# Gates and second modulation as fused products and sums on VectorE, in a transformer block's first heads

## The chip, the cores and the metric

The kernel runs on one core of a Trainium2 chip. The metric is the device time of one execution in microseconds (us), given as the median of repeated runs. A core has five engines with a queue each, served in order: TensorE (PE, matrix products into the PSUM banks), VectorE (DVE), ScalarE (ACT), GpSimd (POOL), and SyncE (SP), which here only issues transfers (DMAs). Semaphores order the queues among each other.

## The reference

One block with adaptive layer norm, for 2 batches of 1024 tokens of width 256, all in float32. From a small vector `c` per batch come six modulation rows: shift and scale of the attention half (`sa`, `ca`), its gate (`ga`), and the same for the feed-forward half.

```
mod = (silu(c) @ wmod).reshape(2, 6, 1, 256)
sa, ca, ga, sb, cb, gb = mod[:, 0..5]
ga = (2*(ga >= 0) - 1) * maximum(abs(ga), 0.25)          # gb likewise
h = layernorm(x) * (1 + ca) + sa
x = x + ga * attention(h)            # 16 heads of 128, rotary q and k, causal softmax, @ Wo + bo
h = layernorm(x) * (1 + cb) + sb
x = x + gb * ffn(h)                  # quantized weights, silu(gate) * up, 704 hidden
```

## The kernel before

The program is one list of instructions in an order written out by hand (`tc.manual_schedule`); each engine takes its own in that order. There are 32 units, one for each batch and head (`units`, two heads to a weight group), and the main loop goes over a unit's eight steps `i`, one for each block of 128 queries. "Head 0" below is the first unit, "head 1" the second, and so on; `n` is the unit's number.

Step `i` of a unit does the following, in this order. `shared_out` projects one token tile of an earlier unit through its output weight and adds it to `x` (`project_out`, L518 on TensorE, L521 on VectorE); it runs 13 steps behind, so unit 0's first tile comes in step 5 of head 1. `score` (L431) multiplies 128 queries with `(i+1)*128` keys into one of two `ps` banks, and VectorE adds the mask there and reduces to the negative maximum (L434, the fused form `tensor_tensor_reduce`, shown as CUSTOM_DVE_ANT_0 and an accumulator read). `turned` (L465) transposes the previous step's probabilities in 32x32 blocks on VectorE; after steps 3 and 7 SP issues 16 DMAs that complete the transposition into `pT` (L477). `expo` (L451) is the exponential on ScalarE. `release` runs what the last `project_qk` held back: VectorE's product with the cosine (L404) and GpSimd's addition (L407). `project_qk` (L388) projects q or k of the next unit; ScalarE adds the bias into a rotated copy `r` (L400, two buffers), GpSimd multiplies it with the sine (L401). `project_v` (L370, two token tiles at a time, copied out by ScalarE L377) and `values` (L492, the product with v into the single `po` bank, copied out by ScalarE L500) follow, then `extras`.

Before the loop stands a prologue. SP and ACT queue the loads; at most eight of these transfers are on their way at a time, since each takes one of eight semaphores in turn and waits until the one before it on that semaphore has landed. x is normalized (`ln_stats`, `ln_sqrt`, `ln_scale`), transposed by TensorE and modulated into `hT` (`ln_turn`, L218, L226 on VectorE, L224 on ScalarE), in two halves of 512 tokens. Between them stand the products of the modulation on TensorE: `modulation(0)` (L125) for the attention half's shift and scale, which lands as columns, and `gates_product` (L149) for both gates, which lands as two rows of 512. `gates` applies sign and lower bound on these rows with four VectorE operations (L155 to L159), writes them to DRAM through SP and reads them back with four broadcasts to 128 partitions. The feed-forward half's `modulation(2)` is done in step 7 of head 0. `fold_out` (GpSimd, L339 to L343) adds a weight group's share of the value bias and multiplies the output weight by the gate; for the first group in step 7 of head 0, before the first `project_out` reads it.

Of the kernel before, what the change touches and what calls it, by code (L numbers as in the profile page):

```python
# [22 lines left out]
KC = D // P  # L23
HG = 2
# [3 lines left out]
QB = 512  # L28
# [9 lines left out]
def adaln_block(ctx: ExitStack, tc: tile.TileContext, a, cos_d, sin_d, out):  # L38
    nc = tc.nc
    pool = lambda name, bufs, **k: ctx.enter_context(tc.tile_pool(name=name, bufs=bufs, **k))  # L40

    const = pool("const", 1)
# [16 lines left out]

    wmod = fpool.tile([P, 2, 2, KC, D], F32, tag="f", name="wmod")  # L60
    wga = fpool.tile([P, KC, 2 * D], F32, tag="f", name="wga")

    def load_x(b, t, n, eng):
        eng.dma_start(x[b][:, t : t + n, :], x_d[b, :, t : t + n, :])

    def load_wmod(block, n, eng):
        eng.dma_start(wmod[:, block, n], a["L0_wmod"][block, n])

# [7 lines left out]
    for n in range(2):  # L76
        load_wmod(0, n, nc.sync)

# [37 lines left out]

    def modulation(which, pool, tag):

        pm = pool.tile([P, 512], F32, tag=tag, name=f"pm{which}")

        wide = pm.rearrange("p (n f r b) -> p n f r b", n=2, f=KC, b=B)
        for n in range(2):
            for f in range(KC):
                for k in range(KC):
                    nc.tensor.matmul(  # L125
                        wide[:, n, f],
                        wmod[:, which // 2, n, k, ts(f, P)],
                        sc[:, :, k].unsqueeze(1).to_broadcast([P, P // B, B]),
                        start=(k == 0),
                        stop=(k == KC - 1),  # L130
                    )
        pms[which] = wide

    pms = {}

    def shift_scale(which):
        pm = pms[which]
        for n in range(2):
            nc.vector.tensor_scalar(modT[:, which + n], pm[:, n, :, 0, :], float(n), None, ALU.add)

    dram = pool("dram", 1, space=bass.MemoryType.DRAM)
    grow_d = dram.tile([B, 2 * D], F32, name="grow_d")

    pgs = []

    def gates_product(k):
        if k == 0:
            pgs.append(ps_y.tile([P, 512], F32, tag="y", name="pg"))
        nc.tensor.matmul(pgs[0][:B], sc[:, :, k], wga[:, k, :], start=(k == 0), stop=(k == KC - 1))  # L149

    def gates():

        pg = pgs.pop()
        sgn = ppool.tile([P, S], F32, tag="p", name="sgn")[:B, :QB]
        nc.vector.tensor_scalar(sgn, pg[:B], 0.0, 2.0, ALU.is_ge, ALU.mult)  # L155
        mag = ppool.tile([P, S], F32, tag="p", name="mag")[:B, :QB]
        nc.vector.tensor_scalar(mag, pg[:B], -1.0, None, ALU.mult)
        nc.vector.scalar_tensor_tensor(mag, pg[:B], 0.25, mag, ALU.max, ALU.max)
        nc.vector.scalar_tensor_tensor(mag, sgn, -1.0, mag, ALU.add, ALU.mult)  # L159
        nc.sync.dma_start(grow_d, mag)  # L160
        for b in range(B):
            for m, n in enumerate(("a", "b")):
                nc.sync.dma_start(
                    gate[n, b], grow_d[b : b + 1, m * D : (m + 1) * D].to_broadcast([P, D])
                )

# [164 lines left out]

    def fold_out(b, g):
        t = weights[b, g]["o"]
        if b == 0:

            for h in range(HG):
                c = R_BV + g * HG + h
                bw = small.tile([P, D], F32, tag="bw", name=f"bw_{g}{h}", bufs=2)
                nc.gpsimd.tensor_scalar(bw, t[:, h, :], cols[:, c : c + 1], None, ALU.mult)  # L339
                nc.gpsimd.tensor_tensor(bvacc, bvacc, bw, ALU.add)  # L340

        for h in range(HG):
            nc.gpsimd.tensor_tensor(t[:, h, :], t[:, h, :], gate["a", b], ALU.mult)  # L343

    gbo = {}
# [14 lines left out]
    weights = {}  # L360
# [150 lines left out]
    def project_out(u, t, late=False):  # L511
# [5 lines left out]
        py = bank(name) if late else ps_y.tile([P, 512], F32, tag="y", name=name)  # L517
# [130 lines left out]
    def extras(n, i):  # L648

        if i == (2 if n else 7) and units[n][2] == 0:  # L650
            fold_out(*units[n][:2])
        if n == 0 and i == 7:
            modulation(2, ps_y, "y")
            shift_scale(2)

# [45 lines left out]
    def shared_out(s, late=False):  # L701
        if s >= 0:
            project_out(units[s // NT], s % NT, late)

    with tc.manual_schedule():
        pc = ps_a.tile([P, 512], F32, tag="a", name="pc")
        nc.tensor.transpose(pc[:, : B * KC], row_c, ident[: B * KC, : B * KC])
        for n in range(2):
            warm_up(4)
        nc.scalar.activation(sc.rearrange("p b k -> p (b k)"), pc[:, : B * KC], AF.Silu)  # L710
        nc.scalar.activation(warm, eps_t, AF.Sqrt)
        weights[0, 0] = {}
        nc.sync.dma_start(wga, a["w_gates"])
        load_w(0, 0, "q")
# [6 lines left out]
        for t, t_d in ((cos_t, cos_d), (sin_t, sin_d)):  # L721
            nc.sync.dma_start(t[:, QB:], t_d[:, QB:])
        for n in range(2):
            load_wmod(1, n, nc.sync)
        load_proj(*units[2][:2])
# [10 lines left out]
        modulation(0, ps_o, "o")  # L736
        ln_scale(0, "a", 0, (0, 1))
        ln_scale(0, "a", 0, (2, 3))
        shift_scale(0)
        ln_turn(0, "a", 0, 0, new_hT(0, 0), split=True)  # L740
        gates_product(0)
        for t in range(4, NT):
# [7 lines left out]
        ln_turn(0, "a", 1, 0, new_hT(0, 1), split=True, wide=True)  # L750
        gates_product(1)
        project_v(0, 0, 2, ps_sc, "sc", S)
        gates()
        for s in ("q", "k"):
# [3 lines left out]
        for n, u in enumerate(units):  # L758
# [5 lines left out]
            for i in range(NT):  # L764

                shared_out(8 * n + i - 13)
                if owed:
# [10 lines left out]
                if i in (6, 7) and prev:  # L778
                    values(prev, 1, 4 * (i - 6), 4 * (i - 5))
                if i in (0, 2):  # L780
                    if h == 0:
                        project_v(b, g, 4 + i, *((ps_a, "a") if n else (ps_o, "o")))
                    elif more:
                        project_v(nb, ng, i)
                if not nxt and i in filler:
                    hidden(0, 0, filler.index(i), late=False, hold=True)

                if prev and i == (0 if n > 1 else 2):
                    values(prev, 0, 0, 4)
                extras(n, i)  # L790
                if i == 7 and h == 1:
# [125 lines left out]
```

## Time and profile before

| what | value |
|---|---|
| median of 3 runs | 1073.14 us (1072.92 to 1076.41) |
| the profiled execution | 1074.62 us |
| its span, first to last instruction | 1072.6 us |
| busy: PE, DVE, ACT, POOL | 1067.6, 656.7, 508.8, 399.2 us |
| granted TensorE clock | 1.00 |
| head 0's first score on TensorE | 23.72 us |
| first scores of heads 1, 2, 3 | 43.58, 71.15, 100.42 us |

All times inside the span count from its first instruction. In a line of a timeline the first number is the start, the second the duration in us, then engine, line of the kernel, operation and operands (out<-in, partitions x elements); "x16" is that many instructions merged, and brackets give the idle time of the engine just before and what ended it. In a line of the groups the numbers behind the bar are the total busy time in us and the mean duration in ns. In a line of the transfers the last number is the time from issue to landing in us. PEld is TensorE's loading of weights, which lies beside the products. Durations of matrix products include the depth of the pipeline; what one occupies is the distance to the next start.

### The profile page before, as it was taken

To read this page: it belongs to the slowest core of one execution; us is meant where nothing else is said; L and a number is where in the kernel's file an instruction comes from. 1 tells how busy PE (TensorE), PEld (TensorE's weight loads), DVE (VectorE), ACT (ScalarE), POOL (GpSimd) and SP (SyncE) were. 2 spreads that over 40 slices of the span, in tenths; PEclk is the share of its full clock that TensorE was granted. 3 is DMA by queue.
4 is the path that set the end of the run, shared out by engine and by line. 5 is a ranking of instruction groups with operands and counts; after the bars stand their busy time and mean duration, and the time that the engine had idled before them with its cause. 6 is when DMAs were issued, how large, how long until landed. Compare 5 with 4: busy or idle time off the path is not lost.

```text
span 1072.6 us, 12387 instructions
## 1 busy us (share of the span) xinstructions
PE 1067.6 (100%) x3513; PEld 638.1 (59%) x3513; DVE 656.7 (61%) x1427; ACT 508.8 (47%) x956; POOL 399.2 (37%) x368
## 2 busy tenths in 40 slices
PE   9999999999999999999999999999999999999998
PEld 5655655665665656556666666656556666545746
DVE  5666675666767776655656656666767756545321
ACT  5654454554445544445544444544555544562110
POOL 4735353534344343754333444334343333200100
PEclk9999999999999999999999999999999999999999
DMA  6465656657564555655464655454655556423201
GB/s 223 102 160 127 160 119 139 159 125 177 118 156 105 142 116 130 135 135 137 110 148 109 148 118 144 100 138 100 143 124 116 147 128 138 110 50 77 71 1 39
DMA packets 68191, 132.02 MB, mean 123 GB/s; under 512 B 19318, under 2 KB 23546, under 8 KB 68124
## 3 DMA queue, kind: packets, MB, share of 16 engines
q1 hardware_dynamic: 66340, 126.83, 50.2%
q10 hardware_dynamic: 1736, 4.29, 1.2%
q8 instruction: 28, 0.46, 0.2%
q14 instruction: 39, 0.32, 0.1%
q0 software_dynamic: 48, 0.13, 0.1%
HBM read 25.26 MB, written 2.10 MB: 26 GB/s over the span
## 4 chain that ended last, share of the span: by engine, by line
PE 98%; DMA 1%; DVE 0%; issue 0%; ACT 0%; POOL 0%; ACTq 0%; POOLq 0%
PE ps L431 23%; PE po L492 23%; PE pk L388 10%; PE py L518 10%; PE pq L388 10%; PE pv L370 10%; PE pgu L547 7%; PE pd L611 3%; DMA s_down<-in_scales 1%; PE warm_ps L88 1%; PE pd L601 0%; PE pm L125 0%; PE ptx_a L218 0%; PE pg L149 0%; DVE ps L434 0%
## 5 line engine op out<-in xcount | busy, mean ns | idle before, releaser
L451 ACT ACTIVATE p<-ps,nmax 128x128 f32<-128x128 f32 (+7 forms) x256 | 190.2, 743 | 343.1 <-DVE nmax L434 342.7
L431 PE MATMUL ps<-kT,qT 128*128 128x512 f32 (+3 forms) x768 | 289.5, 486 | 0.0
L434 DVE CUSTOM_DVE_ANT_0 ps<-ps,mask 128x128 f32<-128x128 f32 (+7 forms) x256 | 195.5, 764 | 112.6 <-PE ps L431 111.6
L492 PE MATMUL po<-pT,v 128*128 128x512 f32 (+3 forms) x768 | 263.5, 486 | 0.0
L521 DVE SCALAR_TENSOR_TENSOR x<-py,rden,x 128x256 f32<-128x256 f32 x256 | 122.8, 481 | 222.6 <-PE py L518 219.0
L492 PEld LDWEIGHTS po<-pT,v 128*128 128x128 f32 x768 | 145.7, 190 | 123.4 <-issue 92.8
L401 POOL TENSOR_TENSOR r_q<-r_q,sin_t 128x512 f32<-128x512 f32 x64 | 81.6, 1275 | 362.8 <-ACT r_q L400 348.4
L465 DVE STREAM_TRANSPOSE t<-p 128x128 f32<-128x128 f32 (+7 forms) x256 | 198.2, 774 | 4.8 <-ACT p L451 3.1
L431 PEld LDWEIGHTS ps<-kT,qT 128*128 128x128 f32 x768 | 145.7, 190 | 77.6 <-issue 64.1
L518 PE MATMUL py<-wo,o 128*128 128x256 f32 x512 | 151.3, 380 | 1.0 <-DVE x L521 1.0
L518 PEld LDWEIGHTS py<-wo,o 128*128 128x128 f32 x512 | 92.5, 190 | 79.0 <-issue 53.3
L370 PE MATMUL pv<-wv,hT 128*128 128x256 f32 x512 | 121.1, 379 | 0.0
L388 PE MATMUL pq<-hT,wq 128*128 128x512 f32 x256 | 120.5, 593 | 0.0
L388 PE MATMUL pk<-hT,wk 128*128 128x512 f32 x256 | 120.4, 592 | 0.0
L370 PEld LDWEIGHTS pv<-wv,hT 128*128 128x128 f32 x512 | 94.8, 190 | 19.5 <-issue 1.3
L401 POOL TENSOR_TENSOR r_k<-r_k,sin_t 128x512 f32<-128x512 f32 x64 | 81.4, 1272 | 64.4 <-ACT r_k L400 64.3
L407 POOL TENSOR_TENSOR kT<-kT,r_k 128x512 f32<-128x512 f32 x64 | 81.2, 1269 | 55.3 <-DVE kT L404 40.7
L400 ACT ACTIVATE r_q<-pq,cols 64x512 f32<-64x512 f32 x128 | 87.6, 684 | 22.2 <-PE pq L388 19.8
L407 POOL TENSOR_TENSOR qT<-qT,r_q 128x512 f32<-128x512 f32 x64 | 83.6, 1307 | 36.9 <-DVE qT L404 30.2
L400 ACT ACTIVATE r_k<-pk,cols 64x512 f32<-64x512 f32 x128 | 87.6, 684 | 6.5 <-PE pk L388 1.0
L388 PEld LDWEIGHTS pk<-hT,wk 128*128 128x128 f32 x256 | 48.6, 190 | 48.2 <-issue 44.5
L388 PEld LDWEIGHTS pq<-hT,wq 128*128 128x128 f32 x256 | 46.2, 190 | 33.1 <-issue 30.6
(94 smaller groups left out, 690.7 us busy)
## 6 DMA issues: line engine op xcount, KB each, us to landing
pT<-t SPq DMA_DIRECT2D x512, 128.0 KB, 2.4
pT<-t SPq DMA_DIRECT2D x512, 64.0 KB, 2.0
wq<-in_Wq SPq DMA_DIRECT2D x16, 256.0 KB, 3.1
wk<-in_Wk SPq DMA_DIRECT2D x16, 256.0 KB, 3.9
wv<-in_Wv SPq DMA_DIRECT2D x16, 256.0 KB, 4.3
wo<-in_Wo SPq DMA_DIRECT2D x16, 256.0 KB, 3.0
out<-yo SPq DMA_DIRECT2D x15, 128.0 KB, 1.8
wmod<-in_wmod SPq DMA_DIRECT2D x4, 256.0 KB, 5.5
```

The source lines that it names most:

```text
L370: nc.tensor.matmul(pv[:, ts(j, HG * DH)], hT[b, n][:, k, ts(r, P)], weights[b, g]["v"][:, k, :], start=(k == 0), stop=(k == KC - 1),)
L388: nc.tensor.matmul(pq, weights[b, g][s][:, k, ts(h, DH)], hT[b, n][:, k, :], start=(k == 0), stop=(k == KC - 1),)
L400: nc.scalar.activation(r1[to], pq[of], AF.Identity, bias=cols[of, c : c + 1])
L401: nc.gpsimd.tensor_tensor(r1, r1, sin_t[:, sl], ALU.mult)
L407: nc.gpsimd.tensor_tensor(dst[:, sl], dst[:, sl], r1, ALU.add)
L431: nc.tensor.matmul(ps[:, c:e], qT[:, ts(i, P)], kT[:, c:e], start=True, stop=True)
L434: nc.vector.tensor_tensor_reduce(ps[:, :L], ps[:, :L], mask[:, NT - 1 - i :, :].rearrange("p t k -> p (t k)"), -SCALE, FLT_MAX, ALU.add, A ...
L451: nc.scalar.activation(p[:, :L], ps[:, :L], AF.Exp, bias=nmax, scale=-1.0, accum_out=dens[u][:, i : i + 1])
L465: nc.vector.transpose(t32[blk][:, :, j, : i + 1, :].rearrange("p c k b -> p k c b"), p[:, : (i + 1) * P].rearrange("p (k c a) -> p k c a", ...
L492: nc.tensor.matmul(po[:, off * P :], vs[b, g][:, k, ts(h, DH)], pT[:, off:, :, k, :], start=(k == 0), stop=(k == last),)
L518: nc.tensor.matmul(py[:, :D], outs[u][:, ts(t, P)], weights[b, g]["o"][:, h, :], start=True, stop=True)
L521: nc.vector.scalar_tensor_tensor(x[b][:, t, :], py[:, :D], rdens[u][:, t : t + 1], x[b][:, t, :], ALU.mult, ALU.add)
```

## The change

Only the attention half's shift and scale are still computed on TensorE. Both gates and the feed-forward half's shift and scale are computed on VectorE as dot products: the weights come transposed (`wmT`, 128 output columns on the partitions, the 256 inputs along them), silu(c) comes as one row broadcast to all partitions (`crow`, through DRAM), and `column` multiplies and sums them with one `tensor_tensor_reduce` of 128x256 for each batch. Eight of these (four `column` calls) make the gates in steps 4 to 7 of head 0, eight more the second modulation in steps 3 and 5 of heads 1 and 2. Sign and bound of the gates are then four operations on 128x8. GpSimd's queue sends these columns to DRAM, where they lie as rows, and reads the rows back with broadcasts in steps 1 (attention) and 5 (feed-forward) of head 1. The value bias share stays in step 7 of head 0, the multiplication of the first output weight by the gate goes to step 4 of head 1.

The first out-projection goes from step 5 to step 7 of head 1, and unit 0's tiles catch up in head 2, two of them through the `po` bank. The v projections of the second weight group's first four tiles go to steps 6 and 7 of head 0 (from steps 0 and 2 of head 1), the later ones to step 0 of heads 1 and 2 (the last two from steps 0 and 2 of head 2), and head 2's first value product goes from step 0 to step 2.

```diff
-    wmod = fpool.tile([P, 2, 2, KC, D], F32, tag="f", name="wmod")
-    wga = fpool.tile([P, KC, 2 * D], F32, tag="f", name="wga")
+    wmod = fpool.tile([P, 2, KC, D], F32, tag="f", name="wmod")
+    late_mod = fpool.tile([P, (4 * KC + B) * D], F32, tag="f", name="late_mod")
+    wmT = late_mod[:, : 4 * KC * D].rearrange("p (w n f k) -> p w n f k", w=2, n=2, f=KC)
+    crow = late_mod[:, 4 * KC * D :].rearrange("p (b k) -> p b k", b=B)
...
-    grow_d = dram.tile([B, 2 * D], F32, name="grow_d")
-    def gates_product(k):
-        if k == 0:
-            pgs.append(ps_y.tile([P, 512], F32, tag="y", name="pg"))
-        nc.tensor.matmul(pgs[0][:B], sc[:, :, k], wga[:, k, :], start=(k == 0), stop=(k == KC - 1))
+    crow_d = dram.tile([1, B * D], F32, name="crow_d")
+    grow_d = dram.tile([B, 2, KC, P], F32, name="grow_d")
+    gcol = const.tile([P, B, 2, KC], F32, name="gcol")
+
+    def column(which, n, f):
+        junk = xnp.tile([P, D], F32, tag="xn", name=f"junk{which}{n}{f}")
+        for b in range(B):
+            to = modT[:, 2 + n, f, b : b + 1] if which else gcol[:, b, n, f : f + 1]
+            nc.vector.tensor_tensor_reduce(
+                junk, wmT[:, which, n, f], crow[:, b], 1.0, float(which * n), ALU.mult, ALU.add, to
+            )
 
     def gates():
...
+        g = gcol.rearrange("p b n f -> p (b n f)")
+        sgn = small.tile([P, 4 * B], F32, tag="sgn", name="sgn", bufs=1)
+        nc.vector.tensor_scalar(sgn, g, 0.0, 2.0, ALU.is_ge, ALU.mult)
...
         nc.vector.scalar_tensor_tensor(mag, sgn, -1.0, mag, ALU.add, ALU.mult)
-        nc.sync.dma_start(grow_d, mag)
-        for b in range(B):
-            for m, n in enumerate(("a", "b")):
-                nc.sync.dma_start(
-                    gate[n, b], grow_d[b : b + 1, m * D : (m + 1) * D].to_broadcast([P, D])
-                )
+        with nc.allow_non_contiguous_dma("columns to rows"):
+            nc.gpsimd.dma_start(grow_d.rearrange("b n f p -> p (b n f)"), mag)
+
+    def gate_rows(n):
+        for b in range(B):
+            row = grow_d[b : b + 1, "ab".index(n)].rearrange("b f p -> b (f p)")
+            nc.gpsimd.dma_start(gate[n, b], row.to_broadcast([P, D]))
...
-        if i == (2 if n else 7) and units[n][2] == 0:
+        if n == 0 and i == 7:
+            bias_share(0)
+        if n == 1 and i in (1, 5):
+            gate_rows("ab"[i // 5])
+        if n == 1 and i == 4:
+            fold_gate(0, 0)
+        if n and i == 2 and units[n][2] == 0:
             fold_out(*units[n][:2])
+        if n == 0 and i >= 4:
+            column(0, *divmod(i - 4, 2))
         if n == 0 and i == 7:
-            modulation(2, ps_y, "y")
-            shift_scale(2)
+            gates()
+        if n in (1, 2) and i in (3, 5):
+            column(1, n - 1, i // 4)
...
         nc.scalar.activation(sc.rearrange("p b k -> p (b k)"), pc[:, : B * KC], AF.Silu)
+        nc.scalar.activation(row_c, row_c, AF.Silu)
+        nc.gpsimd.dma_start(crow_d.rearrange("o (r p) -> (o r) p", p=P), row_c)
         nc.scalar.activation(warm, eps_t, AF.Sqrt)
         weights[0, 0] = {}
-        nc.sync.dma_start(wga, a["w_gates"])
...
+        nc.sync.dma_start(crow.rearrange("p b k -> p (b k)"), crow_d.to_broadcast([P, B * D]))
         for n in range(2):
-            load_wmod(1, n, nc.sync)
+            nc.sync.dma_start(wmT[:, n], a["wmodT"][:, n])
...
-        gates_product(0)
...
-        gates_product(1)
         project_v(0, 0, 2, ps_sc, "sc", S)
-        gates()
...
-                shared_out(8 * n + i - 13)
+                s = 8 * n + i - 13
+                shared_out({0: -1, 1: -1, 2: 0, 3: 1, 4: 2, 5: 4, 6: 5}.get(s, s))
...
                 if i in (0, 2):
-                    if h == 0:
-                        project_v(b, g, 4 + i, *((ps_a, "a") if n else (ps_o, "o")))
-                    elif more:
+                    if n in (1, 2):
+                        if i == 0:
+                            project_v(0, 1, 2 + 2 * n)
+                    elif n == 0:
+                        project_v(b, n, 4 + i, ps_o, "o")
+                    elif h == 0 and n > 2:
+                        project_v(b, g, 4 + i)
+                    elif h and more:
                         project_v(nb, ng, i)
+                if n == 0 and i in (6, 7):
+                    project_v(0, 1, 2 * (i - 6))
...
-                if prev and i == (0 if n > 1 else 2):
+                if prev and i == (0 if n > 2 else 2):
                     values(prev, 0, 0, 4)
+                if s in (4, 6):
+                    project_out(units[0], 3 * s // 2 - 3, pool=ps_o, tag="o")
```

`bias_share` and `fold_gate` are the two halves of `fold_out`; `project_out` takes the pool of its bank as an argument; `modulation` is left with the attention half alone and writes `modT` itself. The host hands over the transposed weights under the name `wmodT`.

More of the change, by code (lines that the diff above doesn't have):

```diff
@@ L58, in adaln_block, with load_wmod @@
     sc = const.tile([P, B, KC], F32, name="sc")
-    wmod = fpool.tile([P, 2, 2, KC, D], F32, tag="f", name="wmod")
-    wga = fpool.tile([P, KC, 2 * D], F32, tag="f", name="wga")
+    wmod = fpool.tile([P, 2, KC, D], F32, tag="f", name="wmod")
+    late_mod = fpool.tile([P, (4 * KC + B) * D], F32, tag="f", name="late_mod")
+    wmT = late_mod[:, : 4 * KC * D].rearrange("p (w n f k) -> p w n f k", w=2, n=2, f=KC)
+    crow = late_mod[:, 4 * KC * D :].rearrange("p (b k) -> p b k", b=B)
     def load_x(b, t, n, eng):
         eng.dma_start(x[b][:, t : t + n, :], x_d[b, :, t : t + n, :])
-    def load_wmod(block, n, eng):
-        eng.dma_start(wmod[:, block, n], a["L0_wmod"][block, n])
+    def load_wmod(n, eng):
+        eng.dma_start(wmod[:, n], a["L0_wmod"][n])
     row_c = rot.tile([P, QB], F32, tag="r1", name="row_c")[: B * KC, :P]
@@ L76, in adaln_block @@
     for n in range(2):
-        load_wmod(0, n, nc.sync)
+        load_wmod(n, nc.sync)
     ident = const.tile([P, P], F32, name="ident")
@@ L115, in adaln_block, with modulation @@
     bvacc = const.tile([P, D], F32, name="bvacc")
-    def modulation(which, pool, tag):
-        pm = pool.tile([P, 512], F32, tag=tag, name=f"pm{which}")
+    def modulation(pool, tag):
+        pm = pool.tile([P, 512], F32, tag=tag, name="pm")
         wide = pm.rearrange("p (n f r b) -> p n f r b", n=2, f=KC, b=B)
@@ L126, in modulation @@
                         wide[:, n, f],
-                        wmod[:, which // 2, n, k, ts(f, P)],
+                        wmod[:, n, k, ts(f, P)],
                         sc[:, :, k].unsqueeze(1).to_broadcast([P, P // B, B]),
@@ L131, in modulation @@
                     )
[L132 to L137, printed above, removed]
         for n in range(2):
-            nc.vector.tensor_scalar(modT[:, which + n], pm[:, n, :, 0, :], float(n), None, ALU.add)
+            nc.vector.tensor_scalar(modT[:, n], wide[:, n, :, 0, :], float(n), None, ALU.add)
     dram = pool("dram", 1, space=bass.MemoryType.DRAM)
-    grow_d = dram.tile([B, 2 * D], F32, name="grow_d")
-    pgs = []
-    def gates_product(k):
-        if k == 0:
-            pgs.append(ps_y.tile([P, 512], F32, tag="y", name="pg"))
-        nc.tensor.matmul(pgs[0][:B], sc[:, :, k], wga[:, k, :], start=(k == 0), stop=(k == KC - 1))
@@ L151, in gates @@
-    def gates():
[L153 to L158, printed above, removed]
+    crow_d = dram.tile([1, B * D], F32, name="crow_d")
+    grow_d = dram.tile([B, 2, KC, P], F32, name="grow_d")
@@ new lines, in adaln_block @@
+    gcol = const.tile([P, B, 2, KC], F32, name="gcol")
[6 more added lines that the diff above has]
+            )
+    def gates():
+        g = gcol.rearrange("p b n f -> p (b n f)")
+        sgn = small.tile([P, 4 * B], F32, tag="sgn", name="sgn", bufs=1)
+        nc.vector.tensor_scalar(sgn, g, 0.0, 2.0, ALU.is_ge, ALU.mult)
+        mag = small.tile([P, 4 * B], F32, tag="mag", name="mag", bufs=1)
+        nc.vector.tensor_scalar(mag, g, -1.0, None, ALU.mult)
+        nc.vector.scalar_tensor_tensor(mag, g, 0.25, mag, ALU.max, ALU.max)
@@ L330, in load_out, with bias_share, fold_gate, fold_out @@
         weights[b, g]["o"] = t
-    def fold_out(b, g):
-        t = weights[b, g]["o"]
[L334 to L340, printed above, removed]
+    def bias_share(g):
+        t = weights[0, g]["o"]
+        for h in range(HG):
+            c = R_BV + g * HG + h
+            bw = small.tile([P, D], F32, tag="bw", name=f"bw_{g}{h}", bufs=2)
+            nc.gpsimd.tensor_scalar(bw, t[:, h, :], cols[:, c : c + 1], None, ALU.mult)
+            nc.gpsimd.tensor_tensor(bvacc, bvacc, bw, ALU.add)
+    def fold_gate(b, g):
+        t = weights[b, g]["o"]
         for h in range(HG):
             nc.gpsimd.tensor_tensor(t[:, h, :], t[:, h, :], gate["a", b], ALU.mult)
+    def fold_out(b, g):
+        if b == 0:
+            bias_share(g)
+        fold_gate(b, g)
     gbo = {}
@@ L509, in bank, with project_out @@
         return pool.tile([P, 512], F32, tag=tag, name=name)
-    def project_out(u, t, late=False):
+    def project_out(u, t, late=False, pool=ps_y, tag="y"):
         b, g, h = u
@@ L516, in project_out @@
         name = f"py_{b}{g}{h}{t}"
-        py = bank(name) if late else ps_y.tile([P, 512], F32, tag="y", name=name)
+        py = bank(name) if late else pool.tile([P, 512], F32, tag=tag, name=name)
         nc.tensor.matmul(
@@ L735, in adaln_block @@
             ln_sqrt(0, "a", t, t + 2)
-        modulation(0, ps_o, "o")
         ln_scale(0, "a", 0, (0, 1))
         ln_scale(0, "a", 0, (2, 3))
-        shift_scale(0)
+        modulation(ps_o, "o")
         ln_turn(0, "a", 0, 0, new_hT(0, 0), split=True)
-        gates_product(0)
         for t in range(4, NT):
@@ L895 @@
     wmod = v["L0_wmod"].reshape(D, 2, 3, D)
-    args["L0_wmod"] = given("in_wmod", by_partition(np.moveaxis(wmod[:, :, :2], 0, 2), 2))
-    args["w_gates"] = given("in_w_gates", by_partition(wmod[:, :, 2].reshape(D, 2 * D)))
+    args["L0_wmod"] = given("in_wmod", by_partition(np.moveaxis(wmod[:, 0, :2], 0, 1), 1))
+    wmT = np.stack([wmod[:, :, 2], wmod[:, 1, :2]]).reshape(2, D, 2, KC, P)
+    args["wmodT"] = given("in_wmodT", wmT.transpose(4, 0, 2, 3, 1))
     gate, up, down = (v[f"L0_ffn_wq_{n}"].T for n in ("gate", "up", "down"))
```

## The prediction

> **What bounds the kernel now.** Read first: the page's busy times and chain; then TensorE's timeline, which shows whether it ever waits.
>
> ```profile
> PE 1067.6 (100%) x3513; PEld 638.1 (59%) x3513; DVE 656.7 (61%) x1427; ACT 508.8 (47%) x956; POOL 399.2 (37%) x368
> PE 98%; DMA 1%; DVE 0%; issue 0%; ACT 0%; POOL 0%; ACTq 0%; POOLq 0%
> 38.57 3.38 PE L431 MATMUL ps<-kT,qT 128*128 128x512 f32 x8
> 41.79 1.95 PE L125 MATMUL pm<-sc,wmod 128*128 128x128 f32 x16
> 43.58 0.39 PE L431 MATMUL ps<-kT,qT 128*128 128x128 f32 x2
> ```
>
> The chain is 98% TensorE, and from 18.46 us to the end of head 3 each group follows the last without a gap (durations overlap by the pipeline's depth). A us taken from TensorE is gained, unless another queue falls behind. VectorE is 61% busy on average; what counts is its free time in head 0, where the new work goes.
>
> **Removed: the second modulation.** 43.58 - 41.79 = 1.79 us of TensorE, all on the path.
>
> **Removed: the gate products and their 512 KB load.** The prologue, from the timeline of all engines:
>
> ```profile
> 9.59 0.81 DVE L226 TENSOR_SCALAR hT<-ptx_a,modT 128x512 f32<-128x512 f32 x1 [0.21 <-PE ptx_a L218]
> 10.86 1.98 PE L388 MATMUL pq<-hT,wq 128*128 128x512 f32 x4
> 13.55 0.43 DVE L188 BATCH_NORM_STATS2 st_a<-x 128x6 f32<-128x256 f32 x1 [0.37 <-DMA x<-in_x]
> 17.51 1.02 PE L149 MATMUL pg<-wga,sc 128*2 128x512 f32 x2
> 18.46 1.99 PE L370 MATMUL pv<-wv,hT 128*128 128x256 f32 x8
> 18.57 0.80 DVE L226 TENSOR_SCALAR hT<-ptx_a,modT 128x512 f32<-128x512 f32 x1
> 20.29 1.02 PE L388 MATMUL pq<-hT,wq 128*128 128x512 f32 x2
> ```
>
> The first product runs 9.91 to 10.77, past the 10.40 at which hT is ready: pq can start at 10.45, 0.41 earlier. The second holds TensorE from 17.51 to 18.46, 0.95 us. But pq at 20.29 also needs hT, which VectorE ends at 19.37; with x arriving as now, only 20.29 - 19.42 = 0.87 is gained in all. That hT (18.57) hangs by ScalarE's order (square root, r_q, r_k) on the last x, which VectorE waits for at 13.55. The load queue is full there (384 GB/s from 6 to 12 us), and wga occupies it about 1.0 us (SyncE's issues that wait for wmod and for wga are at 7.58 and 8.55). With x 1.0 earlier, hT ends at about 18.4 and pq starts at 18.45. Bounds 0.87 and 1.84; I take **1.84**, since the queue is full. Gain so far 1.79 + 1.84 = **3.63**.
>
> **Moved at no net price on TensorE.** Two v projections (1.73 each) leave step 2 of heads 1 and 2 for steps 6 and 7 of head 0; two out-projections (0.43) go from head 1 to head 2; head 2's first value product goes from step 0 to step 2. Of the out-projections that take the po bank (head 2, steps 1 and 3) the first has 1.07 us of TensorE work (0.43 + 0.64) before the bank's next user, against 0.48 for the sum that frees it. wmodT and the c rows enter SP's queue behind the rotary tables, 768 KB more than wmod had there but 512 KB less ahead: the second group's weights land under 1 us later, and are first used 20 us on. SP reaches the c rows at about 9.5, when the GpSimd write (from about 4 us; the DMA below took 3.6) has landed. The Silu of the c row falls in ScalarE's wait for mv (1.20 us); GpSimd's memsets slip some 2 us, and nothing reads them before 27 us. The old gate operations leave VectorE at 19.29 to 22.2, before score 0: nothing. Were a cover gone, each delay would cost its length.
>
> **Added to VectorE.** A column is two fused products of 128x256. The nearest row is the score's reduction of that width, 0.43 us and 0.31 start to start, plus an accumulator read of 0.14: a pair takes 0.9. Four pairs fall in head 0, two each in heads 1 and 2 (before their nmax of steps 4 and 6, in idle time of 1.61 and 0.91). The four small gate operations take about 0.9 with their dependences, up to 1.3 beside GpSimd. In head 0, VectorE idles 0.92 and 0.86 before the reductions of steps 5 and 6, which two pairs eat; the third is covered by the 1.73 of v projection. At the end: score 7 ends at 41.8 - 1.84 + 1.73 = 41.7; reduction to 43.3; transpose to 44.3; pair to 45.2; gates to 46.5; head 1's first reduction and exponential to 47.4. TensorE then does 1.73 + 0.22 + 1.73 + 0.43 + 1.72 = 5.8 us of work to 47.5, where score 2 needs that bank. Late next is step 7's transpose (end 48.0): its 16 transfers, 0.63 apart and 2.4 to land, are there at 60.1, and head 1's step 6 multiplies by them at 60.2. The margin is **0.1** at both: the cover holds barely, and each us more on VectorE in steps 4 to 7 beyond 0.1 (0.9 in steps 4 to 6) is lost.
>
> [...]
>
> ```profile
> 283.74 0.69 DVE L297 SCALAR_TENSOR_TENSOR wdT<-raw_down,sd 128x512 f32<-128x512 int32 x1
> L404 DVE SCALAR_TENSOR_TENSOR kT<-pk,cols,cos_t 128x512 f32<-128x512 f32 x64 | 45.4, 710 | 0.7 <-ACT r_k L400 0.7
> ```
>
> Two SBUF sources take 0.69 and one 0.71. [...] No row has the reducing form with both in SBUF; I take the row.
>
> [...] The same two sources collide with GpSimd, which the trace shows:
>
> ```profile
> 268.16 1.26 POOL L401 TENSOR_TENSOR r_q<-r_q,sin_t 128x512 f32<-128x512 f32 x1
> 268.17 1.80 DVE L297 SCALAR_TENSOR_TENSOR wdT<-raw_down,sd 128x512 f32<-128x512 int32 x1
> 269.49 1.60 POOL L407 TENSOR_TENSOR qT<-qT,r_q 128x512 f32<-128x512 f32 x1
> 352.67 1.27 POOL L407 TENSOR_TENSOR kT<-kT,r_k 128x512 f32<-128x512 f32 x1 [0.58 <-DVE kT L404]
> 352.96 1.13 DVE L204 TENSOR_SCALAR xn_a<-x,mv_a,rstd_a 128x256 f32<-128x256 f32 x1
> 353.90 1.32 POOL L401 TENSOR_TENSOR r_q<-r_q,sin_t 128x512 f32<-128x512 f32 x1
> ```
>
> At 268 VectorE waits out GpSimd (1.80 for 0.69) and GpSimd then waits (1.60 for 1.27). At 353 the waiting VectorE instruction goes ahead of GpSimd's next one, though that is queued. [...] In steps 4 to 6 a column follows the very kT or qT that releases GpSimd's add: the first product is in front[...]. If it gets in before the second product, VectorE loses 1.25 three times, and 0.73 in step 7: 4.5, less the 0.9 of cover, 3.6, and nothing is gained. If the second product, issued 0.31 behind the first and within its 0.43[...], nothing is lost. No row decides; 353 is nearest, where VectorE is the one that goes first, and I take that end.
>
> **The gates' way through GpSimd's queue.** The rows leave SP's queue (where nothing but the first pT waited behind) for GpSimd's. One DMA turns 128x8 columns to rows, 1,024 pieces of 4 bytes, and two pairs of broadcasts wait for it or follow. Behind them stand head 2's rotary adds, behind these ScalarE's r buffers. The nearest row:
>
> ```profile
> L756 POOL DMA_DIRECT2D bo_bc<-in_bo x1 | 0.7, 734 | 0.0
> bo_bc<-in_bo POOLq DMA_DIRECT2D x1, 128.0 KB, 3.6
> ```
>
> That is 128 pieces: 0.73 of GpSimd, 3.6 to landing. Bounds 3.6 and 8 x 0.73 + 2.9 = 8.8; I take 6, between fixed cost and proportion. Issued at about 47.5, landed 53.5; broadcasts 1.5 + 2.9, so 57.9; fold_gate, behind rotary adds, about 62. The first out-projection, delayed by two steps, is at 63.6. The cover is gone at about 7; past it each us costs one, 1.8 at the upper bound.
>
> **Sum.** 3.6 less nothing on the profiled execution: span 1072.6 to 1069.0, execution 1074.6 to 1071.0. That execution is 1.5 over the median of the runs shown, 1073.14; from the median I forecast **1069.6**.
>
> **Rivals and chances.** This kernel's measurement tells about 0.3% (3.2 us) from no change.
> - Cover holds: 0.49. Own range 1069.0 to 1071.0; beyond 0.3% with 0.45, within 0.04.
> - Slower, GpSimd first[...]: head 0, steps 4 to 7. With one of its operations inside each pair, stalls of 3.6 give 1073.1; for it speaks that the add is asked for before the second product. It decides from the fourth lost turn; with two lost turns in each step (5 us more on VectorE) it gives about 1078. Against: row 353. 0.30, of which slower by over 0.3% 0.18, within 0.12.
> - The 1,024 pieces take GpSimd and landing over 10 us: the first out-projection waits, 1073 at 10.6 and 1076 at 13.6. For: pieces of 4 bytes; against: the cover of two steps. 0.13: slower 0.09, within 0.04.
> - Little is gained: x is no earlier (2.7 in all)[...]: 1070.5 to 1072. 0.08: within 0.07, slower 0.01.
>
> Faster 0.45, within 0.3% 0.27, slower 0.28. The range 1068.8 to 1077.0 leaves out some 0.15, mostly of the lost turns.
>
> **What would show it.** Right: no L125 after the prologue, head 0's first score near 21.9, head 1's at 43.4, head 3's near 96.7 for 100.4. Wrong: TensorE idle before head 1's scores 1 and 2 or the v projections of steps 6 and 7, fused products of over 1 us beside GpSimd adds, or the first py waiting for wo.

## The result and the profile after

The changed kernel takes 1081.82 us (median of 6 runs, 1080.08 to 1083.44), the kernel before 1074.6 us beside it (6 runs): ratio 1.007, 95% interval 1.0061 to 1.008. It is **slower by 0.7%**, where 1069.6 was forecast. The profiled execution, the shortest of the six, took 1080.08 us, its span 1078.3, which is 5.7 more than the span of before.

Busy times, chain and two groups of the page of the changed kernel:

```profile
PE 1066.8 (99%) x3493; PEld 636.3 (59%) x3493; DVE 664.1 (62%) x1457; ACT 506.8 (47%) x957; POOL 403.8 (37%) x374
PE 95%; DMA 3%; DVE 2%; ACT 0%; issue 0%; ACTq 0%; SPq 0%
L502 PE MATMUL po<-pT,v 128*128 128x512 f32 (+3 forms) x768 | 265.3, 489 | 5.7 <-DMA pT<-t 5.7
L380 PE MATMUL pv<-wv,hT 128*128 128x256 f32 x512 | 121.2, 380 | 0.7 <-ACT v L387 0.7
```

TensorE still does nearly all of the chain, but it now waits 5.7 us once for transfers of pT and 0.7 for ScalarE, which it did nowhere before. Its timeline, at the places that the prediction named:

```profile
22.89 0.39 PE L441 MATMUL ps<-kT,qT 128*128 128x128 f32 x2
43.81 1.99 PE L380 MATMUL pv<-wv,hT 128*128 128x256 f32 x8 [0.71 <-ACT v L387]
45.64 0.39 PE L441 MATMUL ps<-kT,qT 128*128 128x128 f32 x2
47.92 0.70 PE L441 MATMUL ps<-kT,qT 128*128 128x256 f32 x2 [0.17 <-ACT p L461]
68.95 5.39 PE L502 MATMUL po<-pT,v 128*128 128x512 f32 x8 [5.72 <-DMA pT<-t]
74.17 0.59 PE L528 MATMUL py<-wo,o 128*128 128x256 f32 x2
107.32 0.39 PE L441 MATMUL ps<-kT,qT 128*128 128x128 f32 x2
```

Head 0's first score is 0.83 earlier than before (22.89 for 23.72), head 3's 6.90 later (107.32 for 100.42). The sum between:

| up to head 3's first score | us |
|---|---|
| prologue, gained | -0.83 |
| second modulation, gone from TensorE | -1.79 |
| lost up to head 1's first score (2.06 later, with 3.46 of v projections moved there and 2.62 gained) | +1.22 |
| wait before head 1's value product of step 6 | +5.72 |
| that product itself, 5.39 for 3.60 | +1.79 |
| the rest, 0.6 of it in head 1's steps 0 to 2 | +0.79 |

The value product is longer because the clock falls during the wait (granted 1.00 from 63.3 to 65.5 us, 0.50 from 65.6 to 72.4, with TensorE idle from 63.23 to 68.95); this is it in the kernel before:

```profile
62.98 3.60 PE L492 MATMUL po<-pT,v 128*128 128x512 f32 x8
```

After head 3 the profiled span wins back 1.2; 1.0 of it is one wait for x before an out-projection that this profile of before had and the changed kernel's hasn't.

The last column but two of the windows view is the granted clock, then the DMA engines' busy share and GB/s. Changed kernel:

```profile
52.00:56.00 4.00, 4.00 (x14) 2.19 (x13) 2.75 (x8) 3.11 (x7) 1.26 (x1) 1.00 1.16 117
64.00:68.00 4.00, 0.00 (x0) 0.00 (x0) 0.00 (x0) 1.05 (x2) 2.23 (x3) 0.70 0.95 189
68.00:72.00 4.00, 3.05 (x4) 1.51 (x5) 3.03 (x5) 0.00 (x0) 1.45 (x2) 0.50 0.42 101
```

and the first of these stretches in the kernel before:

```profile
52.00:56.00 4.00, 4.00 (x14) 2.08 (x13) 1.19 (x3) 2.29 (x5) 0.04 (x1) 1.00 0.96 210
```

In both kernels the 16 pT transfers of step 7 run there. The engines are busy nearly or all the time in both (0.96 and 1.16), but move 117 GB/s where they moved 210. What runs beside them is the gates' DMA. Transfers of the changed kernel between 49 and 70 us (last number: issue to landing, median):

```profile
pT<-t SPq DMA_DIRECT2D x16, 128.0 KB, 6.4
ga<-grow_d POOLq DMA_DIRECT2D x2, 128.0 KB, 5.4
grow_d<-mag POOLq DMA_DIRECT2D x1, 4.0 KB, 8.7
```

The same pT transfers before, between 44 and 66 us:

```profile
pT<-t SPq DMA_DIRECT2D x16, 128.0 KB, 2.4
```

Single packets of 4,096 bytes, of median 307 ns and at most 367 before, take up to 3,089 ns between 52 and 58 us. (A piece of the gates' DMA is one element: its record gives 8 x 128 elements of 4 bytes.) The single records of issue and landing tell how the delay adds up. Of the 16 pT transfers the first eight are issued from 50.83 to 55.18, 0.63 apart, and none lands before the gates' columns have (58.37). The issues take eight semaphores in turn, and the ninth, on the first one's, is made only at 58.56, in place of 55.8. Just then GpSimd, which has waited for the columns too, issues the two broadcasts of ga (58.66, 59.25). The last pT transfer is issued at 62.92 and lands after 5.9 us, at 68.81, where TensorE is ready at 63.23.

Besides, pT is asked for late. VectorE and GpSimd in head 0's step 4 of the changed kernel:

```profile
34.60 0.71 DVE L414 SCALAR_TENSOR_TENSOR kT<-pk,cols,cos_t 128x512 f32<-128x512 f32 x1
35.23 0.41 DVE L149 CUSTOM_DVE_ANT_0 junk<-late_mod 128x256 f32<-128x256 f32 x1
35.45 1.32 POOL L417 TENSOR_TENSOR kT<-kT,r_k 128x512 f32<-128x512 f32 x1 [0.53 <-DVE kT L414]
35.57 0.08 DVE L149 DVE_READ_ACCUMULATOR2_ANT gcol<- 128x1 f32 x1
35.68 1.37 DVE L149 CUSTOM_DVE_ANT_0 junk<-late_mod 128x256 f32<-128x256 f32 x1
...
49.52 1.24 DVE L475 STREAM_TRANSPOSE t<-p 128x1024 f32<-128x1024 f32 x1
```

The first product of the pair takes 0.41 us, the second 1.37: it ends at 37.05, just after GpSimd's add, released by the kT sum, has ended (36.77). The same happens in steps 5 and 6 (1.37 beside the adds at 39.47 and 43.76), and the transposition of step 7 begins at 49.52, where it began 4.1 us earlier before:

```profile
45.43 1.25 DVE L465 STREAM_TRANSPOSE t<-p 128x1024 f32<-128x1024 f32 x1
```

So two suspects stand before the wait of 5.7 us: the pieces of 4 bytes, and the lateness that the collisions make.

### The profile page after: what moved, and what is told of

The parts are those of the page before. It is cut to its first block, busy times and chain, and to the rows that moved or that the text cites. A ratio compares the mean times of both kernels' runs of the same rounds, so it can differ in the third digit from the quotient of the medians.

```text
span 1078.3 us, 12374 instructions
## 1 busy us (share of the span) xinstructions
PE 1066.8 (99%) x3493; PEld 636.3 (59%) x3493; DVE 664.1 (62%) x1457; ACT 506.8 (47%) x957; POOL 403.8 (37%) x374
## 4 chain that ended last, share of the span: by engine, by line
PE 95%; DMA 3%; DVE 2%; ACT 0%; issue 0%; ACTq 0%; SPq 0%
PE po L502 23%; PE ps L441 22%; PE py L528 10%; PE pq L398 10%; PE pk L398 10%; PE pv L380 9%; PE pgu L557 7%; PE pd L621 3%; DMA pT<-t 2%; DMA x<-in_x 1%; DMA cols<-in_biases 0%; DVE junk L149 0%; PE pd L611 0%; DVE ps L444 0%; DVE t L475 0%; DVE kT L414 0%
```

## The experiments

| kernel | ratio to before (95%) | TensorE's wait for pT, us |
|---|---|---|
| changed kernel | 1.007 (1.0061 to 1.008) | 5.7 |
| e1_turned | 1.0035 (1.0023 to 1.0048) | 2.3 |
| e2_psum | 1.0048 (1.0033 to 1.0063) | 6.1 |
| e3_crow_late | 1.0079 (1.0061 to 1.0097) | 6.1 |
| e4_before_pieces | 1.0062 (1.0047 to 1.0077) | 4.6 |
| e5_both | 1.0002 (0.9992 to 1.0012) | 2.0 |
| e6_rows_late | 1.0008 (1.0 to 1.0017) | none |
| e7_all | 0.9994 (0.9985 to 1.0003) | 2.2 |
| e8_pieces_early | 1.0 (0.9992 to 1.0009) | none |
| e9_rows_both | 0.9981 (0.9973 to 0.9989) | none |
| e10_tables_late | 0.9969 (0.9957 to 0.998) | none |
| e11_ahead | 1.0074 (1.006 to 1.0088) | 7.1 |

### The pieces of 4 bytes: e1, e4, e8

e1_turned:

```diff
-    grow_d = dram.tile([B, 2, KC, P], F32, name="grow_d")
+    grow_d = dram.tile([32, P], F32, name="grow_d")
...
+    mag32 = const.tile([P, 32], F32, name="mag32")
+    magT = const.tile([P, 32], F32, name="magT")
+    nc.gpsimd.memset(mag32, 0.0)
...
-            nc.gpsimd.dma_start(grow_d.rearrange("b n f p -> p (b n f)"), mag)
+        nc.vector.transpose(magT, mag32)
+        nc.gpsimd.dma_start(grow_d.rearrange("j (c a) -> c j a", a=32), magT)
```

> The gates' 128x8 columns are turned to rows by one VectorE transposition of 32x32 blocks, so that the DMA to DRAM writes pieces of 128 bytes and none of 4 bytes; all else is as in the changed kernel[...]. Theory 'pieces' (the 1,024 pieces of 4 bytes hold the DMA engines while the 16 transfers of head 0's last transposition, pT, want them): the transfers take about 2.4 us each again, the last lands at about 63.2, TensorE waits 0 to 0.5 us before head 1's value product of step 6 in place of 5.7, its clock doesn't fall there, and the time falls by about 7.5 us, from 1081.8 to 1074.3. Rival 'lateness' (the columns' collisions with GpSimd make the transposition of step 7 late, and the wait is theirs): the wait stays at 4 us or more and the time at 1080 to 1082.

Measured: 1077.05 us where before took 1073.06. The wait falls from 5.7 to 2.27 us and the clock no longer falls in the profiled execution. That is the shortest of six (1076.03 us); in four of the others the granted clock is 0.998, so there it still fell for a while. Of e1's transfers from 44 to 72 us, two lines:

```profile
pT<-t SPq DMA_DIRECT2D x16, 128.0 KB, 5.0
grow_d<-magT POOLq DMA_DIRECT2D x1, 16.0 KB, 2.2
```

and its value product on TensorE's timeline:

```profile
66.39 3.67 PE L506 MATMUL po<-pT,v 128*128 128x512 f32 x8 [2.27 <-DMA pT<-t]
```

Four times the bytes land in 2.2 us instead of 8.7. The pieces account for the larger part; but 2.3 us of the wait remain, which neither theory had.

e4_before_pieces and e8_pieces_early put the same kind of DMA into the kernel before, at two places:

```diff
+    dum_d = dram.tile([4 * B, P], F32, name="dum_d")
...
+                nc.gpsimd.dma_start(dum_d.rearrange("r p -> p r"), cols[:, : 4 * B])
```

> The kernel before, with one DMA more: 128x8 elements of the bias columns are written as 1,024 pieces of 4 bytes to a scratch tensor in DRAM, in GpSimd's queue at about 44 us, before the first bias share. Nobody reads it. Theory 'pieces': it lands after 8 to 9 us, the transfers of step 7's transposition (at 45.4 to 46.7) take about 6 us in place of 2.4, the last lands at about 64.5, where the value product wants it at 63.0; TensorE waits about 1.5 us there and the time rises by about 2 us, to 1076.6. Rival 'lateness' (the pieces don't matter by themselves): no wait of TensorE there, and no change within 0.5 us.

> The kernel before with the same additional DMA of 1,024 pieces of 4 bytes as e4_before_pieces, but issued behind the prologue, at about 23 to 25 us, where no pT transfer is under way until head 0's step 4 (about 34). Theory 'pieces cost only by holding up the pT transfers': it lands after 6 to 9 us, nothing waits for it, and the time is that of before, 1073.1, within 0.5. Rival (the pieces cost something wherever they run, by GpSimd's or DRAM's time): 1075 or more.

Measured: e4 1080.1 us (before 1073.06), e8 1073.63 (before 1073.57). e4's transfers between 40 and 56 us:

```profile
pT<-t SPq DMA_DIRECT2D x9, 128.0 KB, 5.7
dum_d<-cols POOLq DMA_DIRECT2D x1, 4.0 KB, 9.7
```

TensorE's timeline of e4:

```profile
55.04 4.09 PE L496 MATMUL po<-pT,v 128*128 128x512 f32 x8 [4.57 <-DMA pT<-t]
```

and e8's transfers between 18 and 44 us:

```profile
pT<-t SPq DMA_DIRECT2D x13, 64.0 KB, 2.0
dum_d<-cols POOLq DMA_DIRECT2D x1, 4.0 KB, 8.9
```

4 KB that nobody reads cost the kernel before 7.0 us at 44 us, nearly what the whole change costs, and nothing at 28 us. The expectation had the effect right, and place and size wrong: the pieces met the transfers of step 3 too, so the wait came at head 1's value product of step 2 (4.57, and 1.77 of lower clock: 4.09 for 2.32). By the records of landing, the last two transfers of step 3, issued at 44.82 and 45.46, landed at 54.38 and 54.58, right behind the pieces (54.20). The pT transfers of step 7 that were issued before that took 5.7 to 7.8 us, those issued after it 2.3 to 2.4. This settles that they cost by what they hold up, neither by GpSimd's time (0.94 to 0.98 us for the issue) nor by their own readers.

### The collisions: e2, e11

e2_psum copies the c rows once to PSUM (ScalarE, head 0's step 1) and reads them there:

```diff
+        if (n, i) == (0, 1):
+            cp = ps_y.tile([P, 512], F32, tag="y", name="crow_ps")
+            nc.scalar.copy(cp, crow.rearrange("p b k -> p (b k)"))
+            cpy.append(cp.rearrange("p (b k) -> p b k", b=B))
...
+        c = crow if which else cpy[0]
...
-                junk, wmT[:, which, n, f], crow[:, b], 1.0, float(which * n), ALU.mult, ALU.add, to
+                junk, wmT[:, which, n, f], c[:, b], 1.0, float(which * n), ALU.mult, ALU.add, to
```

> The c rows that the first head's columns read are copied once to PSUM (the py bank, free until head 1's step 7), so that each of these fused products reads SBUF and PSUM; the DMA of 1,024 pieces is kept. The columns of heads 1 and 2 still read SBUF twice. If the two SBUF sources are what collides with GpSimd, no fused product of head 0 takes over 0.6 us, step 7's transposition starts at about 46.5 instead of 49.5 and head 1's first score at 44.4 instead of 45.6. Theory 'pieces': the wait before head 1's value product of step 6 is only shortened, to about 3.5 us, and the time is about 1077.5. Rival 'lateness': the wait is gone and the time is about 1073. Third case[...]: some fused products still take 1.3 us, and the time stays near 1081.8.

Measured: 1078.51 us (before 1073.06). e2's timeline, first two products of step 4 on VectorE, then the value product on TensorE:

```profile
34.87 0.41 DVE L152 CUSTOM_DVE_ANT_0 junk<-late_mod,crow_ps 128x256 f32<-128x256 f32 x1
35.32 0.42 DVE L152 CUSTOM_DVE_ANT_0 junk<-late_mod,crow_ps 128x256 f32<-128x256 f32 x1
67.10 5.34 PE L505 MATMUL po<-pT,v 128*128 128x512 f32 x8 [6.09 <-DMA pT<-t]
```

No product of head 0 takes over 0.42 us now, and both stalls of TensorE up to head 1's score 1 are gone. The transposition begins 2.6 us earlier (46.91), and still the wait is 6.1, not the 3.5 expected: the pieces start as much earlier (47.08 for 49.70), and TensorE itself arrives 2.2 us earlier (61.01 for 63.23). "Lateness" falls as the cause of that wait. What ends the collisions of the columns with GpSimd is the place of the operand: the second products of steps 4 to 6 took 1.37 with both inputs in SBUF, and 0.42 with one in PSUM. In e2 itself a product of head 2 that still reads SBUF twice took 1.36 beside GpSimd's add (68.94 and 68.71).

e11_ahead leaves both inputs in SBUF and changes the order:

```diff
                 expo(u, i, ps, nmax)
+                if n == 0 and i >= 4:
+                    column(0, *divmod(i - 4, 2))
                 release()
...
-        if n == 0 and i >= 4:
-            column(0, *divmod(i - 4, 2))
```

> As the changed kernel, pieces of 4 bytes included, but head 0's columns stand ahead of the held qT or kT sum of their step on VectorE in place of behind it. Theory: the collision comes from order, since that sum is what releases GpSimd's add; ahead of it GpSimd has no add to do, the second products take 0.4 to 0.5 in place of 1.37, TensorE's stalls in head 0 and at head 1's score 1 go (1.2 us), step 7's transposition starts about 2.5 us earlier, and since the pT wait stays the pieces' (about 6 us, as in e2_psum) the time is about 1079 where the changed kernel has 1081.8. Rival: GpSimd's other products (the sine ones) collide just as well; products over 1 us remain and the time stays above 1081.

Measured: 1081.11 us (before 1073.22). The rival was right by both of its signs: products of over 1 us remain (1.37 and 1.12), and the time stays above 1081. e11's step 5:

```profile
37.60 1.27 POOL L411 TENSOR_TENSOR r_q<-r_q,sin_t 128x512 f32<-128x512 f32 x1
37.78 1.37 DVE L149 CUSTOM_DVE_ANT_0 junk<-late_mod 128x256 f32<-128x256 f32 x1
39.19 0.43 DVE L149 CUSTOM_DVE_ANT_0 junk<-late_mod 128x256 f32<-128x256 f32 x1
39.55 0.75 DVE L414 SCALAR_TENSOR_TENSOR qT<-pq,cols,cos_t 128x512 f32<-128x512 f32 x1
```

Ahead of the sum the second product of steps 4 to 6 is free (0.42 to 0.43), as the theory said, but the first runs into GpSimd's sine product and waits that out. The sums come later too, and with them the banks that they free: TensorE waits 0.22 and 0.58 for them in steps 5 and 6, and from head 0's first score to head 1's it takes 22.85 us, 22.75 in the changed kernel. Order moves the collision (1.37 on the first product in place of the second); the operand's place removes it (0.42 in e2).

### What was left of the wait: e5, e6, e9

e5_both joins the edits of e1 and e2.

> Both repairs at once: the gates turned to rows by one VectorE transposition (no pieces of 4 bytes, as in e1_turned) and the c rows of head 0's columns in PSUM (no collision, as in e2_psum). Theory (the loss has two causes, pieces and lateness, and the gates' broadcasts add a little): the transposition of step 7 ends at about 48.0, its 512 packets with the 64 of ga's rows between them are through by 60 to 61, where the value product wants them at 61; TensorE waits 0 to 0.5 us, no other stall in heads 0 and 1 is left, and what remains are the second modulation's 1.8 us and the prologue's 0.8: 1070.5, beyond 0.3% of noise barely (before: 1073.06). Rival 'something else is lost' (the v projections in steps 6 and 7 or the delayed out-projections have a price of their own): 1072 or more.

Measured: 1074.55 us (before 1073.57). All stalls of head 0 are gone, and TensorE still waits 1.99 us for pT, though the transposition ends at 48.47. Head 3's first score is at 99.74, 0.68 earlier than before: 1.79 and 1.10 gained, 1.99 lost, 0.22 not traced. This profile is the shortest of twelve executions (1072.51 us); the six with a granted clock of 0.998 took 1074.5 to 1076.5, so that the median holds a fall of the clock that the profile doesn't show.

e6_rows_late keeps the collisions of e1 and moves the broadcasts:

```diff
-        if n == 1 and i in (1, 5):
-            gate_rows("ab"[i // 5])
-        if n == 1 and i == 4:
+        if (n, i) in ((1, 4), (2, 1)):
+            gate_rows("ab"[n - 1])
+        if n == 1 and i == 5:
             fold_gate(0, 0)
```

> As e1_turned (no pieces of 4 bytes, the collisions kept), but the broadcasts of ga's rows are issued in head 1's step 4 instead of 1, those of gb in head 2's step 1, and the fold of the gate into the output weights in step 5 instead of 4. In e1_turned TensorE still waited 2.3 us for the last pT transfer. Theory 'broadcasts': the 256 KB of ga's rows, at 55.4 to 60, take their share of the DMA engines from pT; later they don't, the wait is about 1 us and the time about 1075.7 (e1_turned: 1077.05). Rival 'lateness alone' (the transposition ended at 51.65, and 16 transfers at 0.63 with 2.4 to land need until 64 or more in any case): the wait stays at 2 to 2.5 us and the time at 1077.

Measured: 1074.77 us (before 1073.57). e6's transfers from 44 to 72 us, and its value product and first out-projection:

```profile
pT<-t SPq DMA_DIRECT2D x16, 128.0 KB, 2.4
63.27 3.60 PE L506 MATMUL po<-pT,v 128*128 128x512 f32 x8
68.19 0.70 PE L532 MATMUL py<-wo,o 128*128 128x256 f32 x2 [1.32 <-POOL wo L352]
```

With the transposition ending at 50.98, pT is there in time, with no wait; the landing is 2.4 again, against 5.0 in e1 and 4.9 in e5. The remaining wait was that of the 256 KB of ga's rows on the same engines. In e1 the pT transfers behind them take 5.0 to 5.1 us up to the last, which is issued when the rows have landed (61.20 and 60.67): the engines are nearly always busy with pT alone (0.96 before), so that the delay is not made up. Lateness costs nothing at pT. What it costs is the stalls ahead, which delay TensorE as well: from its first score e6 takes 40.4 us to this product, e9 below, without collisions, 38.3. But now the fold is late, and the first out-projection waits 1.32 us for the output weights.

e9_rows_both is e5_both with only the first fold's 128 KB in head 1:

```diff
-        if n == 1 and i in (1, 5):
-            gate_rows("ab"[i // 5])
-        if n == 1 and i == 4:
+        if (n, i) == (1, 4):
+            gate_rows("a", (0,))
             fold_gate(0, 0)
+        if n == 2 and i in (1, 5):
+            gate_rows("ba"[i // 5], (0, 1) if i == 1 else (1,))
```

> As e5_both (no pieces of 4 bytes, the c rows of head 0's columns in PSUM), and of the gates' rows only the 128 KB that the first fold needs are broadcast in head 1, in step 4 in place of 1, with the fold right behind; the other three broadcasts follow in head 2. In e5_both TensorE waited 1.99 us for the last pT transfer while 256 KB of ga's rows passed at 52 to 58 us. Theory 'broadcasts': without them the 16 transfers end by 61, no wait is left in heads 0 to 3, head 3's first score starts at about 97.9 (100.42 before, less 1.79 and 0.83), and the time is that of before less 2.5: 1071, ratio 0.9975. Rival: the wait is only moved, to the fold (the first out-projection waits for the output weights by 1 us or more) or stays at pT; ratio 0.999 or above.

Measured: 1071.3 us (before 1073.22), ratio 0.9981 where 0.9975 was expected. e9's value product comes without a wait, at 60.87:

```profile
60.87 3.60 PE L509 MATMUL po<-pT,v 128*128 128x512 f32 x8
98.14 0.39 PE L448 MATMUL ps<-kT,qT 128*128 128x128 f32 x2
```

The other three broadcasts are not quite free in head 2: its pT transfers of 128 KB took 6.2 us there, and 0.6 us is lost around its value product of step 6 (29.00 us from head 2's first score to head 3's, 28.41 in e5 and e10). That the one makes the other was not tested.

### The prologue: e3, e7, e10

e3_crow_late moves one line (e7_all is e5_both with the same move):

```diff
-        nc.sync.dma_start(crow.rearrange("p b k -> p (b k)"), crow_d.to_broadcast([P, B * D]))
...
         load_out(0, 0)
+        nc.sync.dma_start(crow.rearrange("p b k -> p (b k)"), crow_d.to_broadcast([P, B * D]))
```

> The c rows' DMA (one row of 2 KB read for all 128 partitions) goes from ahead of wmodT to behind the first output weights in SyncE's queue; nothing else is changed. In the changed kernel the DMA engines moved only 130 to 190 GB/s from 9.2 to 11.2 us, right after this DMA was issued at 9.1, with packets of 2 KB at up to 994 ns instead of 84. Theory: these reads of one row hold up the last x. Without them x is there at about 12.4 instead of 13.43, head 0's first score starts at about 21.9 instead of 22.9, and the time falls by up to 1 us, to about 1080.8. Rival: x waits for its own issue at 7.3 and its 6 us of landing whatever is behind it; the first score stays at 22.8 to 22.9 and the time at 1081.8.

> As e5_both, and the c rows' DMA behind the first output weights as in e3_crow_late, where head 0's first score came 0.5 us earlier. All that stands behind head 0 is free of waits, so the 0.5 reaches the end: 1070.0, with head 0's first score at about 22.3. If e5_both still waits for pT, the 0.5 is lost there and the time is e5_both's.

Measured: e3 1081.79 us (before 1073.06), e7 1073.56 (before 1073.57). The last x is there at 12.88 in e3 but at 13.57 in e7, against 13.07 to 14.10 in e1, e2, e5 and the changed kernel; the first scores are at 22.35 and 23.04, against 22.54 to 23.57. The difference of two kernels with the same prologue is as large as what was to be shown, and e3's time is the changed kernel's. So it is not shown that the broadcast of the c rows holds x up.

e10_tables_late is e9_rows_both with the second halves of the rotary tables behind wmodT:

```diff
-        for t, t_d in ((cos_t, cos_d), (sin_t, sin_d)):
-            nc.sync.dma_start(t[:, QB:], t_d[:, QB:])
         nc.sync.dma_start(crow.rearrange("p b k -> p (b k)"), crow_d.to_broadcast([P, B * D]))
         for n in range(2):
             nc.sync.dma_start(wmT[:, n], a["wmodT"][:, n])
+        for t, t_d in ((cos_t, cos_d), (sin_t, sin_d)):
+            nc.sync.dma_start(t[:, QB:], t_d[:, QB:])
```

> As e9_rows_both, and the second halves of the rotary tables (2 x 256 KB) are loaded behind wmodT in place of right behind the last x. In the changed kernel the DMA engines fell to 130 to 210 GB/s from 9 to 11 us, with these tables and the last x under way. Theory 'shared': the last x shares the engines with what is issued behind it, so that it lands at about 12.3 in place of 13.1 to 13.6, head 0's first score comes at about 22.0 and the time is 0.7 us less than e9_rows_both. Rival 'own latency': x lands at 13 or later all the same, the first score is at 22.4 or later and the time within 0.3 us of e9_rows_both.

Measured: 1070.01 us (before 1073.22), ratio 0.9969, interval 0.9957 to 0.998: **faster than both kernels**. e10's chain:

```profile
PE 99%; DMA 0%; DVE 0%; SPq 0%; issue 0%
```

and its timeline, with the statistics of the last x on VectorE and the first scores of heads 0 and 3:

```profile
12.70 0.43 DVE L198 BATCH_NORM_STATS2 st_a<-x 128x6 f32<-128x256 f32 x1
22.16 0.39 PE L448 MATMUL ps<-kT,qT 128*128 128x128 f32 x2
97.16 0.39 PE L448 MATMUL ps<-kT,qT 128*128 128x128 f32 x2
```

VectorE no longer waits for the last x (12.70; 13.09 in e9, where it waited 0.29), and the first score is 0.40 earlier than e9's. The rival's signs all fail, and that points to "shared", but by one profile of each kernel; e3, with the tables in their old place, had 12.88 and 22.35. The whole time is 1.3 less than e9's by the medians of runs taken side by side (14 of e9, 7 of e10; the means differ by 1.2, with a standard error of 0.3). But not all of it is the prologue's: of the 0.98 that the profile is ahead at head 3's first score, 0.40 is from the prologue and 0.59 is the loss in e9's head 2.

## Why the prediction was wrong

- **Second modulation, 1.79**: right. No L129 stands behind the prologue.
- **Prologue, 1.84 taken, 0.83 measured.** The step "I take 1.84, since the queue is full" failed; its lower bound, 0.87, was close to the value. The last x came 0.12 earlier (13.43 for 13.55), not 1.0. Dropping a load of about 1.0 us did not bring its issue 1.0 forward: SyncE stood until an earlier load of x had landed, in both kernels (next issue at 5.97, before at 5.77), and issued the last x at 7.30 for 7.58. It then took about as long to land (6.1 for 5.9), though less lay ahead: from 9.2 to 11.2 us the engines moved 170 GB/s where before they moved 368. With the tables behind it, x came at 12.70 at the latest. Why the packets slow down there was not found. The value itself varies: with this prologue the profiles of seven kernels have their first score at 22.54 to 23.57, with that of before three have it at 23.72 to 24.00.
- **Moved work at no net price**: right. In e10 head 3's first score is at 97.16, and 100.42 - 1.79 - 1.56 (its prologue) is 97.07.
- **The columns' own price**: right, 0.9 a pair. Without a collision a product of 128x256 with both inputs in SBUF takes 0.38 to 0.43 us; the score's reduction of that width, with one in PSUM, takes 0.43.
- **The collision with GpSimd**: the step "I take that end" failed. GpSimd comes between the two products in steps 4 to 6 (its adds start at 35.45, 39.47 and 43.76, the second products at 35.68, 39.70 and 43.99), as the first rival said. The working went wrong at "issued 0.31 behind the first and within its 0.43": the accumulator's read (0.08 us) stands between, and the second starts 0.45 behind, when the first has ended and the add is under way. (That this gap lets the add in is read from the order in the trace; no run closed the gap.) The rival's price was too high: 3.6 us were reckoned, TensorE lost 1.2 up to head 1's first score and 0.6 in the steps behind it. Step 7's pair, reckoned with 0.73, met no collision (0.38 and 0.42).
- **The gates' way through GpSimd's queue**: this step made the sign wrong. Its range for the landing, 3.6 to 8.8, held (8.7), and 6 was too low. But the price was looked for only at the DMA's own readers. The first out-projection waited for no weights; the pT transfers in SyncE's queue, on the same DMA engines, waited instead (6.4 us to land for 2.4). The rival of 0.13 had the right suspect at the wrong place. The sum lacked a term, the load on the shared DMA engines, which was put at nothing: it measured 5.72 of wait and 1.79 of lower clock, of which the broadcasts alone make 2.0 to 2.3 (e1, e5). No run has the pieces without the broadcasts in the changed kernel, so the parts can't be split further. The broadcasts too were entered as latency ("1.5 + 2.9") and not as load. The margin of 0.1 at that very value product stood in the text, without anyone asking what else would be on the engines there.

How the pieces hold the transfers up was not shown. GpSimd's queue has 16 packets of 256 bytes, which is 64 pieces each, and pT packets of up to 3,089 ns lie beside them. How long a packet of pieces holds an engine can't be read from the trace: those 16 are recorded with 0.4 to 0.5 us each.

## What to carry to other kernels

Cost a DMA of few bytes by its pieces and by who shares the DMA engines with it, on every queue, and not by its bytes and its reader: here 4 KB in pieces of 4 bytes took 8.7 us to land and 16 KB in pieces of 128 bytes 2.2, and 4 KB of such pieces that nobody reads cost 7.0 us of the whole time at one place and nothing at another (e4, e8). Ask which transfer with a narrow margin is in flight when it starts. Turn columns to rows on chip first (one VectorE transposition of 0.21 us here), and send large broadcasts when no such transfer is under way (their move took the wait from 2.27 us to none, e1 and e6). Work put into VectorE's gaps beside GpSimd should have one of its inputs in PSUM (products of 0.42 us for 1.37 here, e2); changing the order only moved the collision (e11).

## What the hardware showed unexpectedly

- 1,024 pieces of 4 bytes took 8.7 to 9.7 us to land, and transfers of 128 KB in another queue that were issued meanwhile landed only behind them: after 5.7 to 7.8 us in e4, where nothing else was added, for 2.4. The same columns as 128 rows of 128 bytes took 2.2.
- Two broadcasts of 128 KB alone brought the same transfers from 2.4 to 4.9 to 5.0 us (e1, e5), and the delay stayed up to the last of them.
- Only the longer waits were followed by a lower clock in the profiles: after waits of 2.0 and 2.3 us (e5, e1; mean granted clock of these executions 1.00) the next eight products took 3.67 us for 3.60; after 5.7 to 7.1 us (the changed kernel, e2, e3, e11) they took 5.10 to 5.98. In the changed kernel the granted clock is 0.50 from 65.6 to 72.4 us; the wait began at 63.23. The waits of 4.6 to 7.1 us cost 1.5 to 2.4 us more than their length.
- A wait of about 1 us for x before an out-projection is in the profiles of before, e3 and e6 and in none of the others; the runs of before lie mostly in two groups, 1072.7 to 1073.9 and 1074.4 to 1075.2. This was not followed up.
